# A two-layer graph network with routed experts: answers added in pairs ahead of the transposes, and three expert pages fetched without the page table

## The chip, the cores and the metric

The kernel runs on one core of one Trainium2 chip. The metric is the device time of one execution in microseconds, the median of several runs. The names of the engines in the profile are PE (TensorE matmul), PEld (TensorE weight load), DVE (VectorE), ACT (ScalarE), POOL (GpSimd) and SP (SyncE, which here only issues DMAs).

## What is computed

There are 128 graphs of 64 nodes with 256 features, so 8192 rows, and two layers. Each layer is a graph block and then a block of routed experts. Cut to what matters:

```python
# layer 0: graph part, then 64 experts of 256 x 256, 6 per row
x = x + W2 @ silu(rmsnorm(W1 @ (adjacency @ layernorm(x))))
xn = layernorm(x)
top, idx = top_k(xn @ gate_w.T, 6)
mix = sum_k softmax(top)[k] * (xn @ lattice[idx[k]])         # six "answers" per row
x = x + layernorm(xn + mix @ out_w.T + out_b) * ln_g + ln_b
# layer 1: graph part, then 8 experts 256 -> 512 -> 256, 2 per row
xh = layernorm(x)
h = layernorm(xh) * gamma + beta
x = x + xh + relu((adj @ h) @ W_rel + b_rel + h @ W_root)
xn = layernorm(x)
top, idx = top_k(xn @ Wg + bg + bias, 2)
x = x + sum_k softmax(top)[k] * (relu(xn @ W1[idx[k]] + b1) @ W2[idx[k]] + b2)
```

Everything is in float32.

## The kernel before, in words

The rows are worked on in 32 blocks of 256 (two tiles of 128 rows, T = 2). Four stages follow one another.

1. Layer 0's graph part and its gate. At the end of each block the `Router` r0 sends six copies of each row to a table in DRAM, to the rows that belong to the chosen experts (`send`, L287, indirect DMAs issued by POOL).
2. Layer 0's experts. The table is read in pages of 128 rows of one expert. Each page's result goes to the tensor r0y, the answers, six per row (`reply`, L294).
3. The stage that the change rewrites. For a block, `load3` (L819 to L823) reads the six answers of each row (tile y, two DMAs of 768 KB), xn1, x1 and the adjacency. `mixture` (L833) adds the six answers and turns the sum over at once: 24 transposing matmuls a block, six accumulated in each PSUM region; ACT copies the result (accT, L836). `out_proj` (L841, L844) multiplies by out_w. `layer_out_h` (L850) adds xn1, `layer_out_a` takes the statistics (L45, L46, root on ACT at L36) and adds ln_b to x1 (L856), `layer_out_b` (L862 to L867) normalises h, scales it by ln_g and adds it to x1, then takes the statistics of the sum, and `layer_out_c` makes the two normalised forms on ACT (L884, L888). `flip_h`, `neighbours`, `convolve_a` and `convolve_b` (L897, L905, L913 to L922) are layer 1's graph part. `residual1_a` and `residual1_b` (L928, L938) make the new x and its normalised copy xs, `flip3` and `gate1` (L945, L951) the gate's logits, `choose1` (L957 and the router's L178 to L183), `count1` (L191) and `place1` the place of each row in the table r1x, and `send` (L287 again) writes the rows there.
4. Layer 1's experts. `page_table` (L323 to L371, on DVE) counts the pages of the eight experts from the final counts and writes the start row and expert of each page into r1tab. Then up to 69 pages of 256 rows are worked on: `fetch1` loads the row and expert numbers into SP's registers, and issues the page (px, 258 KB), the first weights (pw, 514 KB) and the bias (128 KB). `flip1` (L76, L1021) turns it, `up` (L1030, L1032) and `down` (L1042 to L1054) apply the expert, and `add` (L302) adds the result to the output in DRAM. Full pages of all experts come first, partly filled ones last. Ahead of that, `fill_end` writes empty rows behind the last row of each expert.

PE, DVE and ACT run in the order in which the program is written; SP's and POOL's instructions are placed by the framework. The order in stages 1 and 3 is written out as a list of pairs (lag, function) for `staggered`: at step s, each function in turn is issued for block s - lag. So a lag of 3 means that a block's function runs three steps after lag 0, and within a step the list's order is the order on each engine. Tiles come from pools; a tile with `bufs=3` has three buffers in turn, and a pool opened after another is closed takes over its memory, so its first writes wait for the last use of the old tiles.

Of the kernel before, what the change touches and what calls it, by code (L numbers as in the profile page):

```python
# [9 lines left out]
F32 = mybir.dt.float32  # L10
# [9 lines left out]
P = 128  # L20
# [58 lines left out]
class Router:  # L79
# [15 lines left out]
    def __init__(self, tc, pool, small, dram, n, D, E, K, T, pg, S, epoch, name, total=None):  # L95
# [46 lines left out]
        self.table = dram.tile([self.spare + pg, self.W], F32, name=name + "x")  # L142
        self.fill(nc.sync, self.spare)

# [21 lines left out]
    def fill(self, engine, row):  # L166
        i = engine.dma_start(
            out=self.table[ds(row, self.pg), :].rearrange("(t p) d -> p t d", p=P),
            in_=self.filler)
        self.alone(i.ins, "fill", "send", "full")  # L170
# [113 lines left out]
    def send(self, row, xs):  # L284
        for t in range(self.T):
            for k in range(self.K):
# [3 lines left out]
                self.alone(i.ins, "send")  # L290
# [18 lines left out]
    def page_table(self, scratch):  # L309
# [29 lines left out]
        v.tensor_scalar(part, part, 0.0, None, op0=ALU.is_gt)  # L339
        v.tensor_tensor_scan(cum, num, self.zero, 0.0, op0=ALU.add, op1=ALU.add)  # L340
# [48 lines left out]
    def needed(self, n):  # L389
# [4 lines left out]
        return v > n  # L394

# [16 lines left out]
def two_layer_gnn_moe_kernel(ctx: ExitStack, tc: tile.TileContext, a: dict, out: bass.AP):  # L412
# [49 lines left out]
    def row_parts(rest, name):  # L462

        part = small.tile([P, D], BF16, name="part", bufs=1)
        out = const.tile([P, 2, D], BF16, name="p_" + name)
        for i in range(3):
            nc.vector.tensor_copy(part, rest)
            nc.vector.tensor_sub(rest, rest, part)
            if i == 0:
                nc.vector.tensor_scalar(out[:, 0, :], part, ident[:, 0:1], None, op0=ALU.mult)  # L470
            else:
                nc.vector.scalar_tensor_tensor(out[:, 0, :], part, ident[:, i:i + 1], out[:, 0, :],
                                               op0=ALU.mult, op1=ALU.add)
        nc.vector.tensor_copy(out[:, 1, :], out[:, 0, :])
        return out
# [316 lines left out]
    fw2 = keep.tile([P, E1, KF, D], F32, name="fw2")  # L792
    with tc.tile_pool(name="c3", bufs=1) as c3, \
# [18 lines left out]
        pg = pmix.tile([P, T, E1], F32, name="pg")  # L812
        r1.begin(counts, work, pmix.tile([P, 2, T, E1], F32, name="pos"))

        def load3(b):
            B = blocks[b]
            B["y"] = y = work.tile([P, T, K0, D], F32, name="y")
            for t in range(T):
                nc.sync.dma_start(out=y[:, t], in_=r0.answer[ts(b * T + t, P * K0), :].rearrange("(p k) d -> p k d", k=K0))  # L819
# [6 lines left out]
        def mixture(b):  # L826
# [3 lines left out]
            for t in range(T):  # L830
                for k in range(KD):
                    for i in range(K0):
                        nc.tensor.matmul(pt[:, k, ts(t, P)], lhsT=B["y"][:, t, i, ts(k, P)], rhs=ident,  # L833
                                         start=(i == 0), stop=(i == K0 - 1), is_transpose=True)
# [22 lines left out]

        def layer_out_b(b):
            B = blocks[b]
            h = B["h"]  # L860
            mv, rs = B["mvh"], B["rsh"]
            nc.vector.reciprocal(rs, rs)  # L862
            B["x2"] = x2 = work.tile([P, T, D], F32, name="x2")
            for t in range(T):
                nc.vector.scalar_tensor_tensor(h[:, t, :], h[:, t, :], mv[:, t, 0:1], ln_g,
                                               op0=ALU.subtract, op1=ALU.mult)
                nc.vector.scalar_tensor_tensor(x2[:, t, :], h[:, t, :], rs[:, t:t + 1], B["x1"][:, t, :],  # L867
                                               op0=ALU.mult, op1=ALU.add)
# [99 lines left out]
        def place1(b):  # L968
            B = blocks[b]
            r1.send(r1.places(b, B["hot"]), B["xs"])  # L970

        staggered(NB, (
            (-2, load3),
            (0, layer_out_h),
            (3, choose1),
            (-1, mixture),
            (1, flip_h),
            (3, count1),
            (2, residual1_a),
            (0, layer_out_a),  # L980
            (-1, out_proj),
            (2, residual1_b),
            (1, neighbours),
            (0, layer_out_b),
            (1, convolve_a),
            (2, flip3),
            (1, convolve_b),
            (2, gate1),
# [7 lines left out]
    with tc.tile_pool(name="wx1", bufs=2) as wx, \  # L996
            tc.tile_pool(name="pt4", bufs=2, space=PSUM) as pt_pool, \
# [3 lines left out]
        pages = [dict() for _ in range(r1.pages)]  # L1001
# [91 lines left out]
```

## Time and profile before

| what | us |
|---|---|
| median of 11 runs (2145.0 to 2152.52) | 2149.57 |
| the profiled execution | 2152.56 |
| its span, first to last instruction | 2150.7 |
| stage 1, to | 610 |
| stage 2, PE from 665 to | 1184 |
| stage 3, first transposes 1219.9, last count ends | 1610.1 |
| stage 4, first transposes | 1622.5 |

| stretch, us | PE busy | DVE busy | ACT busy | granted clock | DMA share |
|---|---|---|---|---|---|
| 0 to 610 | 567.7 | 527.0 | 480.4 | 0.99 | 0.46 |
| 665 to 1184 | 479.5 | 182.2 | 123.4 | 1.00 | 0.75 |
| 1184 to 1220 | 1.2 | 4.7 | 0.0 | 0.57 | 0.30 |
| 1220 to 1610 | 372.3 | 318.2 | 229.1 | 0.97 | 0.75 |
| 1610 to 1622 | 0.1 | 5.4 | 0.0 | 0.50 | 0.31 |
| 1622 to 2150.7 | 512.0 | 116.5 | 180.3 | 0.98 | 0.68 |

How to read the profile: it shows one execution. A group of instructions is a line of the program on one engine with one operation, with its count, busy time and mean duration in ns, and then the idle time of the engine just ahead of it, with what ended that. A timeline row has the start, the time covered, the engine, the line, the operation, the tiles out<-in and the count. Two instructions of an engine can overlap by some tens of ns when the second does not need the first, so durations add up to more than the time; starts do not. Matmuls are pipelined, and their time is best read from the distance of starts. The clock is TensorE's, as granted by the throttle, 1.00 being full speed.

### The profile page before, as it was taken

Reading aid. Unit: us, or ns where it says so; the run is one execution under the profiler, and the core shown is the slowest. Engines: PE = TensorE matmul, PEld = TensorE weight load, DVE = VectorE, ACT = ScalarE, POOL = GpSimd, SP = SyncE. Lnnn points to the kernel's source line nnn. Section 1 sums busy time; section 2 is a strip of 40 time slices with the busy share of each in tenths; the row PEclk is TensorE's granted clock in tenths of the full one; section 3 lists DMA queues with packets and bytes.
Section 4 is the critical chain, followed back from the end, with each engine's and each line's share of the span. In section 5 each row is a group of like instructions: output and inputs, shape, how many; then the busy total and the mean of one; then the engine's idle time right before and its main releaser. Section 6 shows DMA issues by size and latency. Waiting matters only on the chain.

```text
span 2150.7 us, 37354 instructions
## 1 busy us (share of the span) xinstructions
PE 1942.1 (90%) x10563; PEld 1683.9 (78%) x10564; DVE 1185.0 (55%) x3952; ACT 1018.3 (47%) x2037; POOL 1163.6 (54%) x1146
## 2 busy tenths in 40 slices
PE   7999999999936899989898299999978999999997
PEld 5888888888835778877777288888857888888886
DVE  5889999989882333333333178888872222222221
ACT  4888788888821222222222056666643333333332
POOL 0376666666675777777777413333342444444444
PEclk9999999999967999999999699999988999999999
DMA  4244455554367997777765489887726766666765
GB/s 108 93 138 146 149 165 164 164 166 135 127 227 233 273 265 235 208 207 208 207 200 147 164 275 309 269 260 258 258 83 175 170 155 161 160 163 158 163 161 112
DMA packets 284092, 398.93 MB, mean 185 GB/s; under 512 B 56536, under 2 KB 237928, under 8 KB 283888
## 3 DMA queue, kind: packets, MB, share of 16 engines
q1 hardware_dynamic: 204032, 247.67, 40.1%
q0 software_dynamic: 64800, 136.14, 21.1%
q10 hardware_dynamic: 15056, 12.69, 1.8%
q8 instruction: 93, 1.52, 0.3%
q14 instruction: 111, 0.91, 0.2%
HBM read 223.89 MB, written 177.69 MB: 187 GB/s over the span
## 4 chain that ended last, share of the span: by engine, by line
PE 42%; DMA 27%; DVE 13%; POOL 7%; issue 6%; ACT 3%; SPq 0%; ACTq 0%; POOLq 0%; DVEq 0%
DMA r0y<-py_s,px 15%; PE py L1049 8%; PE ph L1030 8%; DMA out_x<-py_s,px 6%; POOL r0x L287 5%; PE py L770 4%; PE ps L833 4%; PE po L844 3%; DVE lat L609 3%; PE pz L905 3%; PE pc L916 3%; DMA r0x<-xs,r0row 2%; DMA px<-r0x 2%; PE ph L599 2%; DVE lat L621 2%
## 5 line engine op out<-in xcount | busy, mean ns | idle before, releaser
L287 POOL DMA_INDIRECT r0x<-xs,r0row x384 | 394.6, 1028 | 258.0 <-issue 170.4
L294 POOL DMA_INDIRECT r0y<-py_s,px x424 | 411.4, 970 | 141.2 <-issue 51.8
L770 PE MATMUL py<-lat,pxT 128*128 x1696 | 409.9, 385 | 39.6 <-DVE py_s L775 25.3
L302 POOL DMA_INDIRECT out_x<-py_s,px x138 | 214.2, 1552 | 316.0 <-DMA out_x<-py_s,px 237.4
L775 DVE TENSOR_SCALAR py_s<-py,px 128x256 f32<-128x256 f32 x424 | 185.7, 480 | 361.5 <-DMA r0y<-py_s,px 153.7
L770 PEld LDWEIGHTS py<-lat,pxT 128*128 128x128 f32 x1696 | 306.6, 191 | 90.3 <-ACT pxT L757 33.2
L757 ACT COPY pxT<-pt 128x512 f32<-128x512 f32 x212 | 123.8, 585 | 429.0 <-PE pt L755 302.3
L1032 ACT ACTIVATE phid<-ph,pw 128x256 f32<-128x256 f32 x276 | 130.7, 474 | 325.7 <-PE ph L1030 201.9
L1030 PE MATMUL ph<-pxT,pw 128*128 128x256 f32 x1104 | 252.0, 382 | 0.8 <-ACT pxT L1021 0.8
L1049 PE MATMUL py<-fw,phid 128*128 x1104 | 250.1, 380 | 0.9 <-issue 0.7
L599 PE MATMUL ph<-lat 128*128 128x256 f32 x1024 | 234.3, 388 | 11.0 <-DVE lat L621 10.3
L632 PE MATMUL ps<-lat 128*128 128x256 f32 x1024 | 237.9, 381 | 0.0
L1030 PEld LDWEIGHTS ph<-pxT,pw 128*128 128x128 f32 x1104 | 211.4, 192 | 30.3 <-ACT pxT L1021 1.2
L599 PEld LDWEIGHTS ph<-lat 128*128 128x128 f32 x1024 | 196.2, 194 | 39.7 <-DVE lat L621 10.0
L1049 PEld LDWEIGHTS py<-fw,phid 128*128 128x128 f32 x1104 | 204.5, 190 | 26.7 <-issue 1.3
L632 PEld LDWEIGHTS ps<-lat 128*128 128x128 f32 x1024 | 193.5, 191 | 24.7
L287 POOL DMA_INDIRECT r1x<-xs,r1row x128 | 129.9, 1015 | 116.2 <-issue 80.4
L755 PE MATMUL pt<-ident,px 128*128 128x128 f32 x848 | 128.4, 275 | 35.7 <-DMA px<-r0x 35.7
L755 PEld LDWEIGHTS pt<-ident,px 128*128 128x128 f32 x848 | 106.5, 142 | 57.8 <-issue 36.2
L1043 DVE TENSOR_SCALAR p<-p 128x2 f32<-128x2 f32 x69 | 11.7, 169 | 238.9 <-ACT p L1042 238.9
L1052 DVE TENSOR_TENSOR py_s<-py,pb 128x512 f32<-128x512 f32 x69 | 47.8, 692 | 162.2 <-PE py L1049 139.4
L833 PE MATMUL ps<-ident,y 128*128 128x128 f32 x768 | 93.4, 280 | 37.4 <-DMA y<-r0y 37.4
(265 smaller groups left out, 2873.2 us busy)
## 6 DMA issues: line engine op xcount, KB each, us to landing
px<-r0x SPq DMA_DIRECT2D x424, 129.0 KB
y<-r0y SPq DMA_DIRECT2D x64, 768.0 KB
pw<-in_L_ffn_W1b SPq DMA_DIRECT2D x69, 514.0 KB
px<-r1x SPq DMA_DIRECT2D x69, 258.0 KB
x<-x SPq DMA_DIRECT2D x64, 256.0 KB
pb<-in_L_ffn_b SPq DMA_DIRECT2D x69, 128.0 KB
r0x<-r0filler ACTq DMA_DIRECT2D x64, 129.0 KB
lat<-in_x SPq DMA_DIRECT2D x32, 256.0 KB
```

Of the source, the lines that this page charges most:

```text
L287: i = self.nc.gpsimd.indirect_dma_start(out=self.table[:, :], out_offset=bass.IndirectOffsetOnAxis(ap=row[:, t, k:k + 1], axis=0), in_=xs[ ...
L294: i = self.nc.gpsimd.indirect_dma_start(out=self.answer[:, :], out_offset=bass.IndirectOffsetOnAxis(ap=x[:, self.D:self.D + 1].bitcast(I32 ...
L302: i, d = f"{self.name}add{i}", self.nc.gpsimd.indirect_dma_start(out=self.total[:, :], out_offset=bass.IndirectOffsetOnAxis(ap=x[:, self.D ...
L599: nc.tensor.matmul(ph[:, c, :], lhsT=w1[:, k, ts(2 * j + c, P)], rhs=B["aggT"][:, k, :], start=(k == 0), stop=(k == KD - 1))
L632: nc.tensor.matmul(B["po"][:, t, :], lhsT=B["hT"][:, c, ts(t, P)], rhs=w2[:, c, :], start=False, stop=(t == T - 1 and c == KH - 1))
L755: nc.tensor.transpose(pt[:, k, ts(q, P)], Q["px", q][:, 0, ts(k, P)], ident)
L770: nc.tensor.matmul(py[:, q, :], lhsT=Q["xT"][:, k, ts(q, P)], rhs=lat[:, ds(regs["e"][(2 * j + q) % 4], 1), k, :].rearrange("p o d -> p (o ...
L775: nc.vector.tensor_scalar(y[:, q, :], py[:, q, :], px[:, 0, D + 1:D + 2], None, op0=ALU.mult)
L833: nc.tensor.matmul(pt[:, k, ts(t, P)], lhsT=B["y"][:, t, i, ts(k, P)], rhs=ident, start=(i == 0), stop=(i == K0 - 1), is_transpose=True)
L1030: nc.tensor.matmul(ph, lhsT=w[:, k * F1 + c * P:k * F1 + (c + 1) * P], rhs=Q["xT"][:, k, :], start=(k == 0), stop=(k == KD - 1))
L1032: nc.scalar.activation(hid[:, c, :], ph, AF.Relu, bias=w[:, KD * F1 + c:KD * F1 + c + 1], scale=1.0)
L1049: nc.tensor.matmul(py[:, t, :], lhsT=Q["hid"][:, c, ts(t, P)], rhs=fw2[:, ds(regs["e"][i % 4], 1), c, :].rearrange("p o d -> p (o d)"), st ...
```

## The change

It has three parts.

*Halved answers.* y has three buffers, and its load is a function of its own (`load_y`), issued a block earlier. A new function `halve` adds answers 3 to 5 to answers 0 to 2 on DVE, one instruction of 2 x 3 x 256 elements, and `mixture` transposes three answers instead of six: 12 matmuls a block.

*A new order in stage 3.* The normalisation of h moves from DVE to ACT (`layer_out_n`, two activations, with a reciprocal and a product on DVE ahead of them), and `layer_out_b` multiplies by ln_g and adds x1 in two instructions of 128 x 512. `gate1` goes from lag 2 near the end of a step to lag 3 at its head; `choose1`, `count1` and `layer_out_b` stand later in the list, and so ACT's copy of `flip3` comes ahead of the roots of `layer_out_b`.

*First pages.* After the sends of block 16, `look` finds for experts 0, 1 and 2 whether 256 rows have been sent to them. If so, that first page is complete: its start row is known, and it is marked as taken. Later sends are put into a group of their own (`late`) that the reads of these pages need not wait for. The pool of stage 4's tiles is opened ahead of stage 3, in memory of its own. Stage 4 begins with these three pages (numbers -3 to -1), whose rows come from `firsts` and whose experts are constants; the page table leaves them out, so the 69 pages are now 3 and 66.

Beside that, the bias rows for PE are kept once and broadcast, rather than stored twice (`row_parts`).

```diff
+    def look(self, m):
+        v = self.nc.vector
+        self.taken = self.pool.tile([P, self.E], F32, name=self.name + "taken")
+        self.firsts = self.pool.tile([P, 4], I32, name=self.name + "firsts")
+        t = self.small.tile([P, m], F32, name=self.name + "look")
+        v.memset(self.taken, 0.0)
+        v.tensor_sub(t, self.run[:, 0, :m], self.base[:, :m])
+        v.tensor_scalar(self.taken[:, :m], t, float(self.pg), None, op0=ALU.is_ge)
+        v.tensor_scalar(t, self.base[:, :m], float(self.spare), None, op0=ALU.subtract)
+        v.tensor_mul(t, t, self.taken[:, :m])
+        v.memset(self.firsts, 0.0)
+        v.tensor_scalar(self.firsts[:, :m], t, float(self.spare), None, op0=ALU.add)
+        self.full_pages -= m
...
     def send(self, row, xs):
+        groups = ("send", "late") if self.taken is None else ("late", "send")
...
-                self.alone(i.ins, "send")
+                self.alone(i.ins, *groups)
...
# page_table
+        if self.taken is not None:
+            assert J == 1
+            v.tensor_sub(full, full, self.taken)
+            v.scalar_tensor_tensor(self.map[:, 0, :], self.taken, float(pg), self.map[:, 0, :],
+                                   op0=ALU.mult, op1=ALU.add)
...
+    def load_first(self, engine):
+        _, v = self.nc.values_load_multi_w_load_instructions(
+            self.firsts[0:1, :], engines=[engine], min_val=0, max_val=self.spare,
+            skip_runtime_bounds_check_because="a first page, or that of zeros")
+        return v
+
+    def fetch_first(self, row, out):
+        d = self.nc.sync.dma_start(out=out, in_=self.table[ds(row, self.pg), :].rearrange("(t p) d -> p t d", p=P))
+        self.tc.declare_no_dep(d.ins, group=self.name + "late", reason="full pages get no rows")
...
+    wx = ctx.enter_context(tc.tile_pool(name="wx1", bufs=2))
     with tc.tile_pool(name="c3", bufs=1) as c3, \
...
+        FIRST = 3
...
+        def load_y(b):
+            blocks[b]["y"] = y = work.tile([P, T, K0, D], F32, name="y", bufs=3)
+            for t in range(T):
+                nc.sync.dma_start(out=y[:, t], in_=r0.answer[ts(b * T + t, P * K0), :].rearrange("(p k) d -> p k d", k=K0))
+
+        def halve(b):
+            y = blocks[b]["y"]
+            nc.vector.tensor_add(y[:, :, :K0 // 2, :], y[:, :, :K0 // 2, :], y[:, :, K0 // 2:, :])
...
# mixture
-                    for i in range(K0):
+                    for i in range(K0 // 2):
                         nc.tensor.matmul(pt[:, k, ts(t, P)], lhsT=B["y"][:, t, i, ts(k, P)], rhs=ident,
-                                         start=(i == 0), stop=(i == K0 - 1), is_transpose=True)
+                                         start=(i == 0), stop=(i == K0 // 2 - 1), is_transpose=True)
...
+        def layer_out_n(b):
+            B = blocks[b]
+            h = B["h"]
+            rs, nm = ops.scale_shift(B["mvh"], B["rsh"])
+            for t in range(T):
+                nc.scalar.activation(h[:, t, :], h[:, t, :], AF.Identity, bias=nm[:, t:t + 1], scale=rs[:, t:t + 1])
+
         def layer_out_b(b):
             B = blocks[b]
             h = B["h"]
-            mv, rs = B["mvh"], B["rsh"]
-            nc.vector.reciprocal(rs, rs)
             B["x2"] = x2 = work.tile([P, T, D], F32, name="x2")
-            for t in range(T):
-                nc.vector.scalar_tensor_tensor(h[:, t, :], h[:, t, :], mv[:, t, 0:1], ln_g,
-                                               op0=ALU.subtract, op1=ALU.mult)
-                nc.vector.scalar_tensor_tensor(x2[:, t, :], h[:, t, :], rs[:, t:t + 1], B["x1"][:, t, :],
-                                               op0=ALU.mult, op1=ALU.add)
+            nc.vector.tensor_mul(h, h, ln_g.unsqueeze(1).to_broadcast([P, T, D]))
+            nc.vector.tensor_add(x2, h, B["x1"])
...
         def place1(b):
             B = blocks[b]
             r1.send(r1.places(b, B["hot"]), B["xs"])
+            if b == NB // 2:
+                r1.look(FIRST)
 
         staggered(NB, (
+            (-3, load_y),
             (-2, load3),
+            (3, gate1),
             (0, layer_out_h),
-            (3, choose1),
             (-1, mixture),
             (1, flip_h),
-            (3, count1),
             (2, residual1_a),
             (0, layer_out_a),
+            (3, choose1),
             (-1, out_proj),
             (2, residual1_b),
+            (0, layer_out_n),
             (1, neighbours),
-            (0, layer_out_b),
+            (3, count1),
+            (-2, halve),
             (1, convolve_a),
             (2, flip3),
+            (0, layer_out_b),
             (1, convolve_b),
-            (2, gate1),
             (3, place1),
             (0, layer_out_c),
             (4, load_w2),
...
+        likely = r1.likely_pages - FIRST
...
         def fetch1(i):
             Q = pages[i]
+            Q["x"] = x = wx.tile([P, 2, W], F32, name="px", bufs=4)
+            if i < 0:
+                if i == -FIRST:
+                    regs["first"] = r1.load_first(ENG.SP)
+                r1.fetch_first(regs["first"][i + FIRST], x)
+                load1(i, i + FIRST)
+                return
...
         stages = (-2, fetch1), (0, flip1), (1, down), (0, up)
-        staggered(r1.likely_pages, stages)
-        with tc.If(r1.needed(r1.likely_pages)):
-            staggered(r1.pages, stages, r1.likely_pages)
+        staggered(likely, stages, -FIRST)
+        with tc.If(r1.needed(likely)):
+            staggered(r1.pages, stages, likely)
```

## The prediction, made before the changed kernel ran

> **What bounds the kernel now.** I read the slices of the page first: TensorE is at 9 tenths nearly everywhere, with three dips (slices 12, 13 and 23, and weakly 30 and 31). They part the span into layer 0's graph part (to 610 us), its experts (665 to 1184), the third stage, which this change rewrites (1220 to 1610), and layer 1's experts (1622 to the end). Then I asked for the busy time of each engine in stretches of the third stage:
>
> ```profile
> core 0: us, PE busy (x) PEld busy (x) DVE busy (x) ACT busy (x) POOL busy (x), PEclk, DMA share, GB/s
> 1350.00:1400.00 50.00, 50.00 (x335) 44.01 (x334) 43.46 (x199) 31.54 (x67) 18.89 (x23) 1.00 0.80 263
> 1400.00:1450.00 50.00, 50.00 (x327) 43.70 (x326) 44.58 (x193) 31.80 (x67) 19.67 (x23) 1.00 0.81 263
> ```
>
> PE is never idle, at a granted clock of 1.00. But weight loads and DVE are both busy 44 of 50 us: two engines near the same limit. The starts of the `mixture` transposes (L833) in the timeline give the step: 1341.3, 1352.6, 1363.9, always 11.29 us. The chain of waits over 1300 to 1622 us runs through PE:
>
> ```profile
> 1352.77 2.67 PE ps L833 x24
> ```
>
> So 24 transposes hold PE for 2.67 us, 0.111 us each. How much room has DVE? The groups of DVE alone, 1300 to 1550 us (22 blocks), answer it:
>
> ```profile
> L850 DVE TENSOR_TENSOR h<-po,xn 128x512 f32<-128x512 f32 x22 | 15.2, 691 | 0.0
> L856 DVE TENSOR_TENSOR x<-x,r_L_ffn_ln_b 128x512 f32<-128x512 f32 x23 | 15.2, 661 | 0.0
> ...
> L957 DVE TENSOR_TENSOR logits<-pg,r_L_ffn_bg 128x16 f32<-128x16 f32 x22 | 3.9, 175 | 12.7 <-PE pg L951 12.7
> ```
>
> The fourth column is idle time ahead of the group. DVE waits for PE in one place only, L957: 12.7 / 22 = 0.58 us a block. Everything else is its own work: 11.29 - 0.58 = **10.71 us a block**. That room of 0.58 us decides the case. The Trainium skill, "Perfetto Trace Analysis", section "Identifying the Most-Contended Engine", says that matmul busy time misjudges TensorE and that its weight loads' busy share is to be held against the other engines' occupancy. By that rule (44 against 44) nothing is gained by moving work from PE to DVE; by the busy column (50 against 44) the step falls with PE's own work, to the 9.96 us worked out next.
>
> **Part 1, the halved answers.** PE loses 12 of 24 transposes a block: 12 x 0.111 = 1.33 us, so PE alone could step at 11.29 - 1.33 = 9.96 us. DVE gains and loses:
>
> - *Removed*: the old `layer_out_b` up to its statistics. Durations overlap where neighbours are independent, so I take starts from the timeline:
>
> ```profile
> 1403.31 0.16 DVE L67 RECIPROCAL bn_rs<-bn_sd 128x2 f32<-128x2 f32 x1
> ...
> 1403.58 0.16 DVE L862 RECIPROCAL bn_sd<-bn_sd 128x2 f32<-128x2 f32 x1
> ...
> 1405.47 0.42 DVE L45 BATCH_NORM_STATS2 bn_st<-x 128x6 f32<-128x256 f32 x1
> ```
>
>  From L862 to the statistics: 1405.47 - 1403.58 = 1.89 us.
> - *Added*: `layer_out_n`'s reciprocal and product, as L67 and L68: 1403.58 - 1403.31 = 0.27. A multiply and an add of 128x512, each waiting for all of the one before: between 0.66 (L856, with a broadcast row) and 0.69 (L850) and a gap, 0.70 each, 1.40. And the halving, an f32 add of 2 x 3 x 256 = 1536 elements. No row has that size; the adds of `square_sum` (L609, SBUF to SBUF) take 0.425, 0.692 and 1.227 us at 256, 512 and 1024 elements, 1.045 ns an element: 1.227 + 512 x 1.045 ns = 1.76, with a gap 1.78. Bounds: 1.2 (the row at 1024) and 2.4 (two of them).
>
>  DVE: 10.71 - 1.89 + 0.27 + 1.40 + 1.78 = **12.27 us**, already above 11.29.
> - *A new wait.* The multiply needs the normalised h, now made on ACT. ACT runs in order, and the two `xs` activations of `residual1_b` stand ahead. The timeline of ACT alone, next to the rows above:
>
> ```profile
> 1403.74 1.52 ACT L938 ACTIVATE xs<-x,bn_nm,bn_rs 128x512 f32<-128x512 f32 x2 [0.60 <-DVE bn_nm L68]
> 1405.17 0.56 ACT L908 COPY z<-pz 128x512 f32<-128x512 f32 x1
> ```
>
>  Count from that function's reciprocal (1403.31): `xs` starts 0.43 later, and gives ACT to the next instruction 1405.17 - 1403.31 = 1.86 later. Two 128x256 activations follow; the pair of L884 of the same form spans 1.09 us in the timeline. So h is ready at 2.95, and with a hand-over (0.03 where DVE idled for a root at 1236.4) the multiply starts at 3.0. DVE arrives at 0.27 + 0.27 + 1.78 = 2.32 and waits 0.68. Behind it stand the multiply and add, x2's statistics, all of `place1` and `layer_out_c`, for which ACT, `flip_h` and the sends wait. Bounds of the wait: 0 and 1.1 (one more pair). I take 0.68. While it lasts, the price of the halving matters little: between 1.2 and 2.4 us the multiply starts at 3.0 all the same.
>
> Step: 12.27 + 0.68 = **12.95 us**, +1.66. PE at 9.96 has slack, and so has ACT: 31.6 of 50 us is 7.1 a block, plus 1.1 for h. Moving `gate1` to the head of the next step removes the 0.58 wait, but DVE is never early enough to use it. Loads of y, one block further ahead, hide behind DVE; that slower step asks less of the DMA (share 0.80 now).
>
> `layer_out_h` starts at 1260.4 for block 3, and `layer_out_c` of block 31 ends at 1588.8: 29 steps at a mean of 11.32. I charge 29 x 1.66 = **+48.1 us**. `look` adds seven small DVE instructions of 0.17: +1.2.
>
> *Head.* DVE's add of the gate's biases (L808) stands ahead of the first halving, and its DMA landed only at 1229.9, an idle time of 13.9 us that cost nothing, since `mixture` of block 0 needed only PE (1219.9). Now it needs two links: halving 1230.1 to 1231.8, then 12 transposes on a half-rate PE (2.4), the copy (0.6) and `out_proj` (2.3): block 0's sum starts at 1237.3 instead of 1230.1, +7.2. The three steps that follow took 30.3 us; by DVE's rows, without the parts not yet begun, they take about 28. Head: **+4.8**, between 0 (biases land earlier) and +10.
>
> **Part 2, the first pages.** Between the stages:
>
> ```profile
> 1609.91 0.20 PE L191 MATMUL pos<-r1hot,r1ones 128*128 128x16 bf16 x2
> ...
> 1616.04 0.17 DVE L371 TENSOR_SCALAR r1tab<-scratch 128x4 int32<-128x4 f32 x1
> ...
> 1618.91 0.40 SPq L397 DMA_DIRECT2D px<-r1x  x1
> ...
> 1622.50 1.09 PE L76 MATMUL pt<-ident,px 128*128 128x128 f32 x4 [12.39 <-DMA px<-r1x]
> ```
>
> PE's last count ends at 1610.1; place, page table, register load and DMA pass before its first flip. Three pages known since block 16, in buffers that wait for no other pool, remove this: their loads (3 x 0.9 MB) can be issued once the last output store is, at about 1601, and land in some 5 us. PE flips at about 1610.2: **-12.3 us**. The page table then hides behind three pages (7.35 us each between L1030 groups); page 0, landed at about 1622, is wanted after 1630. Page count stays 69 (3 + 66), and all later pages step at PE's 7.35, so the shift reaches the end. Bounds: 0 and -16 (the low clock of the first page, whose 16 matmuls took 6.1 us, avoided too). In the tail `residual1_a` no longer stands behind `choose1`: it starts 2.5 us earlier, of which 0.9 is left after the choice that it now precedes: -0.9.
>
> **Sum**: 48.1 + 1.2 + 4.8 - 0.9 - 12.3 = **+40.9**. The profiled execution took 2152.56 us (span 2150.7): 2193.5. The median of the eleven runs, 2149.57, lies 2.99 lower: **2190.5 us**.
>
> **Rivals.**
>
> 1. *ACT is in time.* The step is 12.27: 29 x 0.98 = 28.4 in place of 48.1, **2170.8**. For it: ACT has 4 us of slack a block. Against it: order, not load, makes the wait.
> 2. *The other side: PE sets the pace.* If DVE's 10.71 hides waits on PE that the profile shows as work, they shrink with PE's shorter step. At the limit the step is 9.96: 29 x -1.33 = -38.6 and 48.1 falls away, **2103.8**. It decides from a step of 11.29 + (12.3 + 0.9 - 1.2 - 4.8) / 29 = 11.54 downwards, so 1.4 us a block would have to be hidden. Against it: DVE starts follow one another without gaps over 0.1 us except at L957.
> 3. *The pages don't come early*, because SP issues them in order behind something that waits, or the reads are held by the late sends: no -12.3, **2202.8**.
> 4. *PE's clock falls.* With PE idle a quarter of the time, the gate may act. In the tail it does:
>
> ```profile
> 1584.00:1588.00 4.00, 2.05 (x9) 1.12 (x8) 3.72 (x17) 2.86 (x6) 0.22 (x1) 1.00 0.00 0
> 1592.00:1596.00 4.00, 4.00 (x13) 2.98 (x13) 1.87 (x11) 2.28 (x4) 1.57 (x3) 0.62 0.39 137
> ```
>
>  PE's own work is 9.96 less its waits for ACT (L844 and L951, 11.7 us in 22 blocks, 0.53), 9.4 us. At a clock of 0.62 it would take 15.2 a step, +2.2 over mine: 29 x 2.2 = 64, **2254**. The Trainium skill, "TensorE: Matmul & The Clock Gate", section "What's actually happening", puts the fall after a whole idle window of about 3.4 us; by the rule this rival costs nothing, since the longest idle stretch that I count in the new step (`out_proj` waiting for ACT's copy) is about 1.6 us. The tail's row shows a fall after 4 us with PE half busy.
>
> **Chances.** Forecast 0.62 (its own range 2180 to 2201: the head's bounds, and 0.2 us on the step, 29 x 0.2 = 5.8), rival 1 0.18, rival 3 0.08, rival 4 0.06, rival 2 0.04, and 0.02 for no change. The range 2160 to 2212 takes in rivals 1 and 3 with the head's bounds. A measurement of this kernel tells 0.2% from no change: faster 0.04, same 0.02, slower 0.94.
>
> **What would show it.** Right: `out_proj` and `mixture` step at about 13 us; DVE's busy share in the third stage near 95%, PE's near 75%; the multiply idles about 0.7 us for ACT's h in each block; the halving takes 1.76 us; the first flip follows the last count within 1 us. Wrong: a step below 11.5, an add of 1536 elements near 1 us, or a first flip that still comes after the page table.

## The result, and the profile after

The changed kernel takes 2196.67 us (median of 8 runs, 2195.41 to 2202.81). The kernel before, run beside it on the same chip, takes 2149.68 (31 runs). The ratio is 1.0224 with a 95% interval of 1.0213 to 1.0234: slower by 47.0 us. The forecast was 2190.5, with a range of 2160 to 2212. The profiled execution took 2197.0 us, its span 2195.2.

Two points cut the span into pieces that both kernels have. One is the start of `layer_out_h` of block 3, when the pipeline of stage 3 is full. The other is `layer_out_c` of the last block, number 31. The steps are the distances between the starts of `layer_out_h`, and their median is given. The sum of the forecast stands beside each piece:

| piece, us | before | after | difference | forecast |
|---|---|---|---|---|
| up to `layer_out_h` of block 3 | 1260.4 | 1268.8 | +8.4 | +4.8 |
| block 3 to `layer_out_c` of block 31 | 328.2 | 373.4 | +45.2 | +48.1 + 1.2 |
| (median step) | 11.29 | 12.84 | +1.55 | +1.66 |
| to the end of the last count | 21.5 | 21.6 | +0.1 | -0.9 |
| to the first flip of stage 4 | 12.4 | -0.1 | -12.5 | -12.3 |
| stage 4 | 528.2 | 531.6 | +3.4 | 0 |
| sum | 2150.7 | 2195.2 | +44.5 | +40.9 |

The busy time of each engine, in the same stretches of the third stage that were shown of the kernel before:

```profile
core 0: us, PE busy (x) PEld busy (x) DVE busy (x) ACT busy (x) POOL busy (x), PEclk, DMA share, GB/s
1350.00:1400.00 50.00, 42.37 (x244) 34.36 (x243) 44.28 (x171) 31.27 (x67) 15.61 (x20) 0.97 0.71 231
1400.00:1450.00 50.00, 42.71 (x245) 34.64 (x243) 44.16 (x173) 30.25 (x66) 15.59 (x20) 0.97 0.69 228
```

PE fell from 50.0 to 42.5 of 50 us, and weight loads from 44 to 34.5. DVE stayed at 44.2, although each block now has more work on it: the step became longer instead. From these columns alone no engine looks like a limit, and 44.2 of 50 reads like room. The groups of DVE alone, 1300 to 1550 us (20 blocks; the fourth column is idle time ahead of the group, and what ended it), show where the rest is:

```profile
L855 DVE TENSOR_TENSOR y<-y 128x1536 f32<-128x1536 f32 x20 | 35.2, 1759 | 0.5 <-issue 0.5
...
L908 DVE TENSOR_TENSOR h<-h,r_L_ffn_ln_g 128x512 f32<-128x512 f32 x20 | 13.8, 692 | 12.7 <-ACT h L902 12.7
...
L998 DVE TENSOR_TENSOR logits<-pg,r_L_ffn_bg 128x16 f32<-128x16 f32 x19 | 3.2, 168 | 0.0
```

L855 is the halving, 1.759 us. L998 is the sum of the logits (L957 before), at which DVE used to wait 0.58 us a block for PE: 0.0 now. In its place DVE waits at L908, the multiply by ln_g, for the h that ACT normalises at L902: 12.7 / 20 = 0.64 us a block. The timelines of DVE and of ACT, around the same point of one block (start, us covered, engine, line; in brackets the idle time before and who ended it):

```profile
1415.20 0.16 DVE L67 RECIPROCAL bn_rs<-bn_sd 128x2 f32<-128x2 f32 x1
...
1415.75 1.76 DVE L855 TENSOR_TENSOR y<-y 128x1536 f32<-128x1536 f32 x1
1418.18 0.69 DVE L908 TENSOR_TENSOR h<-h,r_L_ffn_ln_g 128x512 f32<-128x512 f32 x1 [0.67 <-ACT h L902]
```

```profile
1415.64 1.52 ACT L979 ACTIVATE xs<-x,bn_nm,bn_rs 128x512 f32<-128x512 f32 x2 [2.13 <-DVE bn_rs L67]
1417.07 1.08 ACT L902 ACTIVATE h<-h,bn_nm,bn_rs 128x256 f32<-128x256 f32 x2
```

DVE gives both pairs of scale and shift within 0.6 us, does the halving, and is done at 1417.51. ACT was idle for 2.13 us beforehand, so it does not lack time. It takes the two `xs` activations first, because `residual1_b` stands ahead in the list, and h comes second. The multiply starts 1418.18 - 1415.20 = 2.98 us after the reciprocal.

At the head of stage 3, on DVE:

```profile
1229.63 0.17 DVE L840 TENSOR_TENSOR r_L_ffn_bg<-r_L_ffn_bg,r_L_ffn_bias 128x8 f32<-128x8 f32 x1 [15.19 <-DMA r_L_ffn_bias<-in_L_ffn_bias]
...
1230.39 3.43 DVE L855 TENSOR_TENSOR y<-y 128x1536 f32<-128x1536 f32 x2 [0.51 <-DMA x<-x]
1238.44 0.69 DVE L889 TENSOR_TENSOR h<-po,xn 128x512 f32<-128x512 f32 x1 [4.63 <-PE po L883]
```

The add of the gate's biases (L808 before) waits 15.19 us for its DMA, and the first halvings stand behind it. And at the seam between stages 3 and 4, on PE:

```profile
1663.54 0.20 PE L207 MATMUL pos<-r1hot,r1ones 128*128 128x16 bf16 x2
1663.60 1.09 PE L76 MATMUL pt<-ident,px 128*128 128x128 f32 x4
```

The first page is turned directly behind the last count. On SP's queue the three pages were issued long before, at 1490.68, soon after `look` (1485.9):

```profile
1490.68 1.86 SPq L426 DMA_DIRECT2D px<-r1x  x3
```

### The profile page after: what moved, and what is told of

It is laid out like the page before. It is cut to its first block, busy times and chain, and to the rows that moved or that the text cites. A ratio compares the mean times of both kernels' runs of the same rounds, so it can differ in the third digit from the quotient of the medians.

```text
span 2195.2 us, 36685 instructions
## 1 busy us (share of the span) xinstructions
PE 1925.8 (88%) x10180; PEld 1650.1 (75%) x10180; DVE 1233.9 (56%) x3958; ACT 1045.2 (48%) x2101; POOL 1163.2 (53%) x1146
## 5 line engine op out<-in xcount | busy, mean ns | idle before, releaser
L1106 PE MATMUL py<-fw,phid 128*128 (+1 forms) x1104 | 250.1, 380 | 0.8 <-ACT phid L1088 0.3
L630 PE MATMUL ph<-lat 128*128 128x256 f32 x1024 | 232.0, 385 | 11.0 <-DVE lat L652 10.3
L1086 PEld LDWEIGHTS ph<-pxT,pw 128*128 128x128 f32 x1104 | 211.5, 192 | 30.3 <-ACT pxT L1077 1.1
L1100 DVE TENSOR_SCALAR p<-p 128x2 f32<-128x2 f32 x69 | 12.1, 176 | 225.3 <-ACT p L1099 225.3
L654 ACT ACTIVATE lat<-lat,c_L_gnn_rms_weight 128x256 f32<-128x256 f32 x256 | 105.6, 494 | 36.8 <-DVE lat L652 36.4
```

Source lines behind the costliest of these rows:

```text
L630: nc.tensor.matmul(ph[:, c, :], lhsT=w1[:, k, ts(2 * j + c, P)], rhs=B["aggT"][:, k, :], start=(k == 0), stop=(k == KD - 1))
L1086: nc.tensor.matmul(ph, lhsT=w[:, k * F1 + c * P:k * F1 + (c + 1) * P], rhs=Q["xT"][:, k, :], start=(k == 0), stop=(k == KD - 1))
L1106: nc.tensor.matmul(py[:, t, :], lhsT=Q["hid"][:, c, ts(t, P)], rhs=fw2[:, ds(e, 1), c, :].rearrange("p o d -> p (o d)"), start=(c == 0), s ...
```

## The experiments

**How the runs are read.** The first four kernels ran on a chip where the kernel before takes 2150.4 us. The other eight ran on two chips where stages 1 and 2 took some 300 us longer in every profile (the first load of y was issued at 1497 to 1512 us, not at 1213 to 1216), and where the kernel before took 2481.07 and 2486.3. Stages 3 and 4 look as usual there. So for every kernel I give the time from the issue of the first load of y to the end of the span, which leaves stages 1 and 2 out. It is one execution each; stage 4 alone varies between 523.5 and 532.0 in these profiles.

| kernel | first load of y to `layer_out_h` of block 3 | median step | block 3 to 31 | to last count | seam | stage 4 | first load to end |
|---|---|---|---|---|---|---|---|
| before | 46.5 | 11.29 | 328.2 | 21.5 | 12.4 | 528.2 | 936.8 |
| after | 55.8 | 12.84 | 373.4 | 21.6 | -0.1 | 531.6 | 982.3 |
| pages_alone | 48.2 | 11.29 | 328.2 | 21.5 | -0.1 | 523.7 | 921.4 |
| stage3_alone | 56.1 | 12.83 | 371.9 | 20.2 | 12.1 | 525.0 | 985.3 |
| no_halving | 46.8 | 12.83 | 373.1 | 21.0 | -0.1 | 523.5 | 964.3 |
| h_first | 55.6 | 12.07 | 350.4 | 18.9 | -0.1 | 530.6 | 955.4 |
| dve_norm | 53.1 | 12.25 | 353.9 | 18.6 | -0.1 | 528.0 | 953.5 |
| dve_norm2 | 53.0 | 12.25 | 353.9 | 18.6 | -0.1 | 529.5 | 954.9 |
| bias_late | 48.0 | 12.85 | 373.9 | 20.5 | -0.1 | 532.0 | 974.2 |
| bias_late2 | 49.4 | 12.84 | 373.6 | 21.5 | -0.1 | 529.9 | 974.3 |
| pool_hfirst | 60.1 | 13.93 | 390.8 | 21.5 | -0.1 | 524.6 | 996.9 |
| one_pair | 57.3 | 11.44 | 333.6 | 20.5 | -0.1 | 526.2 | 937.5 |
| one_pair2 | 56.9 | 11.45 | 333.8 | 20.4 | -0.1 | 525.7 | 936.7 |
| six_h_first | 48.0 | 11.44 | 334.5 | 21.5 | -0.1 | 527.1 | 930.8 |

The theory under test is the forecast's: in the full pipeline the step is DVE's row of work plus its wait for h, and that wait comes from ACT's order. The rivals are that the halving itself is the price, or PE's order, or the pages.

**pages_alone.** The changed kernel with stage 3 put back: six transposes, `layer_out_b` on DVE, the old list. Only the first pages are left of the change (and the broadcast bias rows).

```diff
-            (-3, load_y),
+            (-2, load_y),
             (-2, load3),
-            (3, gate1),
...
-            (-2, halve),
...
+            (2, gate1),
...
-                    for i in range(K0 // 2):
+                    for i in range(K0):
```

> Stage 3 as in the kernel before (six transposes, old order, old layer_out_b), with the first pages, look and the pool opened early. If the two parts of the change simply add up, stage 3 steps at 11.29 us and the first flip of stage 4 follows the last count at once, 12.4 us earlier than before: 2149.7 - 12.4 + at most 2 for look and for stage 4's own waits, 2137 to 2140. If the gain at the seam is given back in stage 4 (the 3.4 us by which stage 4 took longer in the changed kernel being a consequence of the early pages), about 2141; if the early fetches get in the way of stage 3's loads, near 2149.

Measured: 2139.6 us (11 runs), ratio 0.9953 [0.9937, 0.9969]. The step is the old one and the seam is gone:

```profile
1613.77 0.20 PE L207 MATMUL pos<-r1hot,r1ones 128*128 128x16 bf16 x2
1613.82 1.09 PE L76 MATMUL pt<-ident,px 128*128 128x128 f32 x4
```

So the first pages do what they are for, and this part alone beats both kernels. The gain in the median, 10.8 us, is a little below the seam's 12.5.

**stage3_alone.** The reverse: the new stage 3 with the old stage 4 and no `look`.

```diff
-            if b == NB // 2:
-                r1.look(FIRST)
...
-        staggered(likely, stages, -FIRST)
+        staggered(r1.likely_pages, stages)
```

> Halving, new order and row_parts of the change, with stage 4, its pool and its page table as in the kernel before. Additive: 2196.7 + 12.4 = 2209, step of stage 3 12.84 us, a wait of about 12 us between the last count and the first flip. If the early pool and the first pages cost stage 3 something (their memory, look, the loads), the step is below 12.84 and the time below 2205.

Measured: 2202.58 us (4 runs), ratio 1.0247 [1.0221, 1.0273], step 12.83. Stage 3 alone brings the loss. The 2209 expected is missed by 6.4 us, and the time lies below the 2205 named as a sign that the first pages cost stage 3 something; the step gives no such sign, 12.83 against 12.84. The two parts add up to the whole within 6 us: +52.2 here and -10.8 there make +41.4, and the whole is +47.0. The table shows where such a difference can come from: `look`'s step, a tail 1.4 us longer, and a stage 4 that took 531.6 after the change and 525.0 and 523.7 in these two.

**no_halving.** The changed kernel without `halve`; six answers are transposed again. It keeps the new order.

```diff
-            (-2, halve),
...
-                    for i in range(K0 // 2):
+                    for i in range(K0):
```

> The changed kernel without halve: six answers are transposed again, the new order and ACT's normalisation stay. Theory, that the multiply's start is set by ACT (xs, then h) and not by the halving's length: DVE loses 1.78 us of work but waits for h 2.4 us in place of 0.67, and the step stays at 12.8 us; only the head gets shorter, by up to 8 us, since mixture of block 0 no longer waits for DVE: 2188 to 2197. Rival, that the added pass on DVE is the price: the step falls to PE's 11.29, 29 x 1.55 = 45 us less, about 2150.

Measured: 2180.61 us (one run), step 12.83. That is the step of the changed kernel, to 0.01 us, with 1.76 us less work on DVE and twice as many transposes on PE. DVE's multiply, 1300 to 1550 us, shows where the 1.76 went:

```profile
L908 DVE TENSOR_TENSOR h<-h,r_L_ffn_ln_g 128x512 f32<-128x512 f32 x19 | 13.2, 692 | 44.6 <-ACT h L902 44.6
```

44.6 / 19 = 2.35 us of waiting a block, against 0.64 with the halving: 1.71 more. The wait took the place of the work. So in the full pipeline the halving costs nothing and ACT's order sets the pace. What this kernel does save is at the head (46.8 in place of 55.8). The whole time fell below the 2188 to 2197 expected: beside the 9.0 at the head, stage 4 took 523.5 us and not 531.6, which is not the step's doing.

**h_first.** The changed kernel with one line of the list moved, so that ACT makes h ahead of `xs`.

```diff
-            (2, residual1_b),
             (0, layer_out_n),
+            (2, residual1_b),
```

> The changed kernel with layer_out_n ahead of residual1_b in the list, so ACT makes h before xs. Theory: the multiply finds h ready, the step falls by the whole wait, 0.67 us, to 12.17, 2196.7 - 30 x 0.67 = 2177. Rival: the wait only moves (xs is a microsecond later, and flip3, z or the sends wait for it instead), step 12.5 or more, 2187 or more.

Measured: 2170.54 us (2 runs), ratio 1.0100 [1.0068, 1.0132], step 12.07. The wait is gone, and DVE is busy 46.5 of 50 us:

```profile
L908 DVE TENSOR_TENSOR h<-h,r_L_ffn_ln_g 128x512 f32<-128x512 f32 x21 | 14.4, 685 | 0.0
```

```profile
1350.00:1400.00 50.00, 44.68 (x255) 35.24 (x256) 46.45 (x180) 32.98 (x70) 17.10 (x20) 1.00 0.82 263
```

Two lines swapped give back 26.1 us of the 47.0, more than the 20 expected: the step is 0.1 shorter than the 12.17 foreseen, and the tail 2.7 us. What is left, 12.07 against 11.29, is DVE's own work.

**dve_norm and dve_norm2.** The normalisation of h stays on DVE (the old `layer_out_b`); halving and the rest as changed. The second is the same kernel on another chip.

```diff
-            (0, layer_out_n),
...
-            nc.vector.tensor_mul(h, h, ln_g.unsqueeze(1).to_broadcast([P, T, D]))
-            nc.vector.tensor_add(x2, h, B["x1"])
+            nc.vector.reciprocal(rs, rs)
...
+                nc.vector.scalar_tensor_tensor(h[:, t, :], h[:, t, :], mv[:, t, 0:1], ln_g,
+                                               op0=ALU.subtract, op1=ALU.mult)
+                nc.vector.scalar_tensor_tensor(x2[:, t, :], h[:, t, :], rs[:, t:t + 1], B["x1"][:, t, :],
+                                               op0=ALU.mult, op1=ALU.add)
```

> The changed kernel with the old layer_out_b (two times two scalar_tensor_tensor on DVE, no layer_out_n): halving, new order and first pages stay. From the measured starts of the changed kernel: 12.84 less the product's 0.27, the wait 0.67 and multiply plus add 1.45, plus the old function's 1.89: step 12.34, about 2197 - 30 x 0.5 = 2182. If the wait on ACT was not a loss (DVE would have waited elsewhere), 12.84 and 2197.

> The kernel dve_norm again, on another chip: the normalisation of h stays on DVE as before, the halving is there. Step 12.25; blocks 3 to 31 353.9 in place of 373.4 (-19.5), head -2.7, tail -2.9, stage 4 0 to -3: 2170 us (2167 to 2174). Rival (the halving alone, without a wait for ACT, leaves the step as it was): 2197.

Measured: steps of 12.25 in both; from the first load to the end 953.5 and 954.9, that is 28.8 and 27.4 us less than the changed kernel. (The whole times, 2459.11 and 2466.08 us, are of the chips with the longer stages 1 and 2, so the second expectation's 2170 us cannot be held against them; 2197.0 - 27.4 = 2169.6 would answer to it.) Keeping the work on DVE is as good as moving it to ACT with the right order (955.4): the move to ACT saves DVE 0.18 us a block and costs the order.

**bias_late and bias_late2.** The changed kernel with the add of the gate's biases taken from ahead of stage 3 into `choose1` of block 0, three steps later.

```diff
-        nc.vector.tensor_add(bg, bg, gbias)
...
         def choose1(b):
             B = blocks[b]
+            if b == 0:
+                nc.vector.tensor_add(bg, bg, gbias)
```

> The changed kernel with DVE's sum of the gate's two bias rows moved from the head of stage 3 into choose1 of block 0. Theory: the first halving no longer stands behind a DMA that lands at 1229.6, and starts when y lands (about 1223); block 0's sum is at about 1232 instead of 1238.4, and 2197 - 6 = 2191. Rival: the answers and the small rows share the same DMA engines, the sum stays near 1236, and the time within 2 us of 2197.

> The kernel bias_late again, on another chip: the changed kernel with the sum of the gate's biases moved from ahead of stage 3 into choose1 of block 0, three steps later. Theory (the first halving waits behind that sum for its DMA, and what is lost at the head is kept): h of block 3 comes 47.9 after the first load of y in place of 55.8, 2196.7 - 7.7 = 2189.0 us, ratio 1.018 to the kernel before. Rival (what the head gains is given back in a later wait): 2196.7, ratio 1.022.

Measured: `layer_out_h` of block 3 comes 48.0 and 49.4 us after the first load, not 55.8; blocks 3 to 31 take what they took; the totals are 974.2 and 974.3, 8 us less than 982.3. The changed kernel itself was profiled on another chip; on these two, one_pair and one_pair2, which still have the add ahead, come at 57.3 and 56.9. What is won at the head is kept. By the whole times the ratios to the kernel before are 1.000 [0.9984, 1.0016] and 0.9983 [0.9965, 1.0001] on those chips, not the 1.018 expected; the paragraph behind one_pair's comes back to that. The head is not free of waits even so. On DVE of bias_late2, the first two halvings (L854 in this kernel):

```profile
1518.23 1.76 DVE L854 TENSOR_TENSOR y<-y 128x1536 f32<-128x1536 f32 x1 [7.71 <-DMA m_L_gnn_W_root<-in_L_gnn_W_root]
1524.58 1.76 DVE L854 TENSOR_TENSOR y<-y 128x1536 f32<-128x1536 f32 x1 [4.59 <-DMA y<-r0y]
```

The first comes 9.3 us after its load was issued (1509.0), the second waits for its own y.

**pool_hfirst.** The halving goes to POOL, which is busy 16 to 19 of 50 us; h ahead of `xs` as in h_first. If the load on DVE alone counted, the step would be PE's.

```diff
-            nc.vector.tensor_add(y[:, :, :K0 // 2, :], y[:, :, :K0 // 2, :], y[:, :, K0 // 2:, :])
+            nc.gpsimd.tensor_add(y[:, :, :K0 // 2, :], y[:, :, :K0 // 2, :], y[:, :, K0 // 2:, :])
```

> As h_first, with the halving on POOL, which has 34 of 50 us free. Theory: DVE's step is 12.07 - 1.78 = 10.3, PE's 9.96, so 10.3 to 10.6; 2170.5 - 30 x 1.6 = 2122, a little less for the head. Rival: POOL's add is much slower than DVE's or stands in its in-order queue behind sends that wait for DVE, so mixture waits for it: step 11.3 or more, 2150 or more.

Measured: 2505.35 us where the kernel before takes 2481.07, ratio 1.011 [1.0079, 1.014]; steps between 11.3 and 16.3, median 13.93; the longest of all from the first load to the end, 996.9. POOL's add takes 3.43 us, and DVE stands still in the middle of an instruction while it runs. POOL, then DVE, in one block:

```profile
1702.62 3.43 POOL L855 TENSOR_TENSOR y<-y 128x1536 f32<-128x1536 f32 x1
```

```profile
1702.38 0.16 DVE L68 SCALAR_TENSOR_TENSOR bn_nm<-bn_mv,bn_rs 128x2 f32<-128x2 f32 x1
1702.46 0.16 DVE L67 RECIPROCAL bn_rs<-bn_sd 128x2 f32<-128x2 f32 x1
1702.65 3.42 DVE L68 SCALAR_TENSOR_TENSOR bn_nm<-bn_mv,bn_rs 128x2 f32<-128x2 f32 x1
1706.10 0.16 DVE L922 TENSOR_TENSOR bn_rs<-bn_rs,one 128x2 f32<-128x2 f32 x1
```

A product of two numbers per row takes 0.16 us just before, and 3.42 us when it starts 0.03 us after POOL's add; it ends 0.02 us after it. In the profile such time counts as busy, not as a wait. From block 3 on, the ten steps in which hardly anything is held (under 0.25 us over the usual durations) take 11.3 to 11.7 us; the others are longer by about the time that DVE is held in them, up to 16.35 us with 5.0 held. So it is this that makes the move worse than the halving on DVE, and a busy column can't tell it from work. Even the steps without it are above the 10.3 to 10.6 of the theory, for there DVE waits again for h, 17.2 / 18 = 0.96 us a block (1650 to 1900 us):

```profile
L908 DVE TENSOR_TENSOR h<-h,r_L_ffn_ln_g 128x512 f32<-128x512 f32 x18 | 12.5, 693 | 17.2 <-ACT h L902 13.4 <-issue 3.8
```

The paragraph on six_h_first says why. The last section has more on the held instructions.

**one_pair and one_pair2.** DVE adds only the sixth answer to the first (an add of 2 x 256 elements), PE transposes five; h ahead of `xs`. This divides the work otherwise: 0.70 us on DVE for four transposes.

```diff
-            nc.vector.tensor_add(y[:, :, :K0 // 2, :], y[:, :, :K0 // 2, :], y[:, :, K0 // 2:, :])
+            nc.vector.tensor_add(y[:, :, :1, :], y[:, :, :1, :], y[:, :, K0 - 1:, :])
...
-                    for i in range(K0 // 2):
+                    for i in range(K0 - 1):
```

> As h_first, but DVE adds only the sixth answer to the first (2 x 256 elements, 0.69 us), and PE transposes five, 20 matmuls a block. DVE 12.07 - 1.78 + 0.71 = 11.0 us, PE 11.29 - 4 x 0.111 = 10.85: a step of 11.0 with both nearly full, 2170.5 - 30 x 1.07 = 2138. Where two full engines wait for each other each step (ACT between them), 11.3 or more, 2147.

> The kernel one_pair again, on another chip: DVE adds only the sixth answer to the first, PE transposes five, h ahead of residual1_b. The run before gave 0.987 of the kernel before, on a chip where stages 1 and 2 took some 300 us longer, while its own stages 3 and 4 account for less. By the stages: first pages alone 2139.6, head +9.1 (its h of block 3 came 57.3 after the first load of y, 48.2 with the pages alone), +5.4 for steps of 11.44, tail -1: 2153 us (2149 to 2158), ratio 1.000 to 1.003. Rival (the ratio 0.987 was the kernel's): 2122.

Measured: steps of 11.44 and 11.45, and 937.5 and 936.7 us from the first load to the end: 15 to 16 more than pages_alone, the first halving's delay at the head (57 against 48) and 5.5 us of steps among it. PE is busy 48.5 of 50 us and DVE 45.1, and DVE still waits for h, 5.4 / 18 = 0.30 us a block. The step is no shorter than before, and not by PE's doing, as the paragraph on six_h_first shows. No way of dividing the sum that was tried makes the step shorter than 11.29; one pair with the normalisation kept on DVE was not run.

By the whole times the ratios are 0.9871 [0.9839, 0.9902] and 0.9845 [0.9799, 0.9891], on the two chips with the longer stages 1 and 2. The second expectation took the first of these for the chip's doing, not the kernel's, and foresaw 1.000 to 1.003; by the ratio it missed, since the run fell on such a chip again. Of the time that the profiles show, stages 3 and 4 take what the kernel before's take (936.8), and yet the kernel before takes 32 and 41 us longer than one_pair there (2481.07 - 2448.94 and 2486.3 - 2445.41). No profile of the kernel before was taken on those chips, so where it loses them is open: in its stages 1 and 2, which the change hardly touches, or in a stage 3 and 4 that run otherwise there. The same shift of some 40 us stands in bias_late's ratios. I therefore use no ratio of those chips as a verdict on a part of the change, except to compare kernels of the change with each other.

**six_h_first.** No halving, and h ahead of `xs`: DVE has room, PE its 24 transposes.

```diff
-            (2, residual1_b),
             (0, layer_out_n),
+            (2, residual1_b),
...
-            (-2, halve),
```

> Leaves out the halving (six answers are transposed again, 24 transposes) and issues the h activations ahead of residual1_b; the rest is the changed kernel. DVE: 12.27 - 1.78 = 10.5 us a block, PE as in the kernel before. Theory (the step is what the slower of PE's order and DVE's row of work needs, and DVE now has room): the step is PE's again, 11.0 to 11.3, the first halving's delay at the head is absent (1.4 us less than with the first pages alone), the tail 1 us shorter: 2137 us (2128 to 2141), seam -0.1. Rival (the new order of the list by itself costs PE something, whatever DVE does): a step of 11.6 or more, 2148 or more.

Measured: step 11.44, above the 11.0 to 11.3 of the theory and below the 11.6 of its rival; 930.8 us from the first load to the end. 2436.66 us is 8.8 less than one_pair2 on the same chip. PE is busy 49.7 of 50 us, and DVE waits 17.3 / 18 = 0.96 us a block at the multiply:

```profile
1640.00:1690.00 50.00, 49.69 (x324) 43.11 (x324) 42.52 (x188) 35.07 (x76) 18.20 (x21) 1.00 0.89 292
```

```profile
L908 DVE TENSOR_TENSOR h<-h,r_L_ffn_ln_g 128x512 f32<-128x512 f32 x18 | 12.5, 692 | 17.3 <-issue 10.4 <-ACT h L902 6.9
```

By its column PE looks like the limit again, but it is not what sets this step. one_pair has 20 transposes and not 24, and takes the same 11.44; so do the steps of pool_hfirst in which DVE is not held, with 12. DVE's row without the halving, 10.48 by no_halving, and its wait of 0.96 make just this. This wait is a loop between DVE and ACT. In one block, DVE and then ACT:

```profile
1672.96 0.16 DVE L67 RECIPROCAL bn_rs<-bn_sd 128x2 f32<-128x2 f32 x1
...
1674.53 0.69 DVE L908 TENSOR_TENSOR h<-h,r_L_ffn_ln_g 128x512 f32<-128x512 f32 x1 [0.95 <-issue]
```

```profile
1673.40 1.09 ACT L902 ACTIVATE h<-h,bn_nm,bn_rs 128x256 f32<-128x256 f32 x2 [1.83 <-DVE bn_nm L68]
```

ACT was idle for 1.83 us and makes h as soon as DVE has given its scale and shift; h is done at 1674.49, and DVE has only some 0.6 us of work until it needs it. In this order, then, with h on ACT, DVE's row and this wait hold the step at 11.44, however few transposes PE has. That is where the 0.15 us above 11.29 come from.

With h first, then, the halving turns a step of 11.44 into 12.07: +0.63 us, since the rest of it fits into the wait. With `xs` first it costs nothing, because DVE waits for ACT longer than the halving takes. What a removed instruction is worth depends on the order around it.

## Why the prediction was right, and where its terms were off

*The mechanism.* The forecast said that DVE has 0.58 us of room a block, that the change puts more on it than that, and that ACT's order adds a wait. All three are in the trace. DVE's wait for PE is 0.0. DVE's row of work was put at 12.27; h_first, which has it without the wait, steps at 12.07. The wait was put at 0.68 and is 0.64. The multiply was to start 3.0 us after the reciprocal and starts after 2.98. The sentence that the price of the halving matters little while the wait lasts is shown by no_halving, where the price is zero and the step the same: its step less its wait, 12.83 - 2.35 = 10.48, is the forecast's row of work without the halving, 12.27 - 1.78 = 10.49.

*The step* was 0.11 us too long in the forecast (12.95 against 12.84): in the changed kernel the row is 12.84 - 0.64 = 12.20, 0.07 below the 12.27, and the wait 0.04 below. In h_first the row is 12.07, 0.2 below. The terms of the change itself hold: from the reciprocal to the statistics of x2 they were to take 4.40 us and take 4.43 (1415.20 to 1419.63). What is too high is the 10.71 taken over from the old order; dve_norm, with the old `layer_out_b` and the halving, says the same, 12.25 where 10.71 + 1.78 is 12.49. With `look`'s step, 13.73 (0.89 us over the median; +1.2 was charged), the stretch was forecast at +49.3 and measured at +45.2: 4.1 too much.

*The head* was the term that was mis-sized: +8.4 in place of +4.8, inside its bounds. Block 0's sum comes 8.4 us later (7.2 forecast). The larger part of the miss is the three steps behind it: they were to take 28 us instead of 30.3, "by DVE's rows, without the parts not yet begun", and took 30.3 again. DVE's rows leave out its waits. In these steps DVE idles for ACT's roots, ACT's h and PE, the seven waits of over 0.3 us together 4.8 us, for instance

```profile
1256.59 0.17 DVE L67 RECIPROCAL bn_rs<-rs 128x2 f32<-128x2 f32 x1 [0.78 <-ACT rs L36]
...
1264.77 0.69 DVE L908 TENSOR_TENSOR h<-h,r_L_ffn_ln_g 128x512 f32<-128x512 f32 x1 [0.63 <-ACT h L902]
```

In the full pipeline (blocks 5 to 25) the roots cost DVE no such wait: apart from the one for h, its waits of over 0.15 us add up to 0.03 us a block. The cause that the forecast named, the add of the biases ahead of the first halving, is shown by bias_late: without it the head is 6 to 8 us shorter.

*The tail* was to gain 0.9 and lost 0.1. In h_first and dve_norm the same piece takes 18.6 to 18.9, but in six_h_first, which also has h first, 21.5, and bias_late gave 20.5 and 21.5 in two runs. What decides it is not settled.

*The seam*: -12.5 against -12.3, with the pages issued 173 us before they are used.

*Stage 4* was to shift as a whole, and took 3.4 us longer. It has 8 pages that take over 7.5 us, and had 6. But such pages number 1 to 10 in kernels with the same stage 4, and their stage 4 takes 523.5 to 532.0. The early pages alone do not bring them: pages_alone has one and takes 523.7. Whether the different end of stage 3 or the execution decides is not settled.

*The base*: the profiled execution of before lay 2.99 above the median that the forecast started from, and that of the changed kernel only 0.3. This makes 2.7 of the 6.2 us by which the forecast was low; the terms make the rest (3.6 + 3.4 + 1.0 - 4.1 - 0.2, but for rounding). Errors of both signs stand in this sum, so that the total came this close is in part luck.

*What was to show it.* DVE was foreseen near 95% and PE near 75%; they are at 88% and 85%. My figures for DVE came from starts, which include the gaps between instructions, and the column does not. PE's column grew: 42.5 of 50 us is 10.9 a block, where the old step less twelve transposes gave 9.96. Groups that now wait for ACT show longer instructions (1300 to 1550 us: `out_proj`'s products 448 ns on average, 392 before; `flip_h`'s 300, 273 before); why was not tested.

*The rivals.* ACT in time (12.27): h_first shows nearly that step (12.07) when it is in time, and that in the changed kernel it is not. PE setting the pace: no, PE idles 1.9 us a block, waiting for ACT's results (37.2 us in 20 blocks, at accT, z and hn). Pages not early: the seam says they are. The clock: 0.97 in these stretches with PE idle 15% of the time, and the step follows DVE's row and wait, not PE.

## What to carry to other kernels

When two engines are near the same limit, work that one loses and the other gains moves the limit; read each engine's room from its waits a block, not from its busy share, before deciding where an operation goes. When an operation is moved to an engine that has time, its place in that engine's order can count more than its length: here two lines of a list were worth 26 us, and the 1.76 us halving nothing in the step. Where kernels with very different work take the same step (11.44 with 24, 20 and 12 transposes), look for a loop of waits and not for the busiest engine. Part a change into pieces that can stand alone, since the seam's gain (10.8 us) was hidden under a loss five times its size.

## What the runs showed of the hardware that was not expected

POOL's add of 1536 elements with both operands in SBUF takes 3.43 us, where DVE takes 1.76, and holds some of DVE's instructions until it ends. In pool_hfirst, 1650 to 1900 us, the means of whole groups grow; the products of two tiles in L293 from 193 ns (in the changed kernel) to 1062, the add of L895 from 658 to 1039:

```profile
L855 POOL TENSOR_TENSOR y<-y 128x1536 f32<-128x1536 f32 x18 | 61.8, 3435 | 1.4
...
L293 DVE TENSOR_TENSOR r1prod<-r1hot,r1place 128x32 f32<-128x32 bf16 x18 | 19.1, 1062 | 0.6
L895 DVE TENSOR_TENSOR x<-x,r_L_ffn_ln_b 128x512 f32<-128x512 f32 x18 | 18.7, 1039 | 0.0
```

Not all of them: instructions of DVE that began while POOL added and read one tile in SBUF, or one in SBUF and one in PSUM, kept their times (statistics 0.41 us, reciprocals 0.16, the add of h from PSUM 0.68). Those that read two tiles in SBUF did not, nor did the cast of the chosen experts' numbers (0.17 us otherwise, up to 3.48) and one subtraction of `look`'s (L155, 0.17 in the changed kernel, 3.39 here). The Trainium skill, "SBUF — State Buffer", section "Who interferes with whom", has the rule: a VectorE instruction with two SBUF inputs, or in a 2-port mode, contends with a GpSimd instruction that reads SBUF, and whichever comes second is blocked until the first ends. The trace agrees: 3.42 us beside an add of 3.43.
